# Statistics of the first 30 blocks summed on ACT and POOL, and the first pair's turn and keys ahead of the norm

## The chip, the core and the metric

The kernel runs on one core of one Trainium2 chip. The metric is the device time of one launch in microseconds (us), from start to end of the program on that core. Three runs of the kernel before took 2647.06, 2650.92 and 2656.12 us; the median is 2650.92. One further execution was recorded by the hardware profiler, and all views of the profile below come from it.

The engines are named as the profile names them: PE is TensorE (matmuls; PEld its weight loads), DVE is VectorE, ACT is ScalarE, POOL is GpSimd, and SP is SyncE, whose queue issues the transfers. Each engine runs its own instructions in order and waits on semaphores for the others.

## The reference

The input x has 256 rows of 256 positions of 128 channels. Two layers each add something to x. Only the head of the first one matters here:

```python
def _gn(v, G=32, eps=1e-5):
    B_, H_, W_, C_ = v.shape
    g = v.reshape(B_, H_, W_, G, C_ // G)
    m = jnp.mean(g, axis=(1, 2, 4), keepdims=True)
    s = jnp.var(g, axis=(1, 2, 4), keepdims=True)
    return ((g - m) / jnp.sqrt(s + eps)).reshape(v.shape)
...
q = split_heads(jnp.einsum('...qi,oi->...qo', q_x, wq)) / np.sqrt(C_HIDDEN)
k = split_heads(jnp.einsum('...ki,oi->...ko', kv_x, wk))
v = split_heads(jnp.einsum('...ki,oi->...ko', kv_x, wv))
a = jnp.einsum('bshqd,bshkd->bshqk', q, k)
a = a + bias1 + bias2
a = jax.nn.softmax(a, axis=-1)
...
x = x + _L0_conv_ref(_gn(x), L0_conv_kv_x, L0_conv_bias1, ...)
```

The group norm `_gn` needs the mean and variance of groups of 4 channels over all of x, 32 MB, before the first query can be made. Keys and values come from `kv_x` and need no norm. The second layer (an operator made of Fourier transforms, with norms of its own) follows on the result; the change doesn't touch it.

## The kernel before, in words

`layer0` does the first layer in two stages.

**Reading for the statistics.** x is read in 32 blocks of 1 MB (`xb`, line 140, four buffers; line 141 issues the transfer on SP). PE turns each block by transposes into four PSUM tiles of 128 channels by 512 (line 145, six buffers), and DVE takes a mean and a variance of each tile (`bn_stats`, line 146): 128 tiles in all, kept in `stats`. A tile's entry has six numbers: count, mean and sum of squared deviations of its even and of its odd elements. After block 2 the weights come: lines 148 to 153 issue their transfers on SP between those of the blocks (two buffers for the raw weights, so that SP waits for PE before it loads wv, wg and wo), PE transposes them (line 155) and ACT copies them. After block 8 `prepare` does the same with the two biases: bias1 is loaded into the still unused big array `U` (line 248), PE transposes it (line 255), ACT takes its exponential (line 259), POOL scales it (line 260). At the end `load` (line 277) issues the first two pairs of rows: eight transfers of 64 KB for each, four of x and four of kv.

**The norm.** DVE puts the 128 entries together (`bn_aggr`, line 166), a matmul with `gavg` averages over each group (line 50), ACT copies the mean (line 51), DVE works out the channel variances around it (lines 53 to 55), a second matmul averages those (line 57), ACT copies, and `rsqrt` follows: DVE adds eps (line 35), ACT takes a square root (line 37; a table of functions has to be loaded into ACT first), DVE inverts and improves it (lines 38 to 43). `fold` (lines 231 to 240) multiplies the query and gate weights with the result (`wn`, line 237) and makes their constants `qb` and `hbg` with two small matmuls (line 238).

**The loop over rows.** `run` writes the order of all engines out by hand: within `manual_schedule` each engine's instructions keep the order in which the program names them. Rows go in pairs. `turn` (line 303, DVE) transposes a pair of x and kv rows in squares of 32; `project` (PE line 295, ACT line 318) makes queries and keys of a row; `values` makes the values of a pair (ACT line 326) and the gate's sums; `gates` takes tanh (line 333); `scores` does the row's scores (PE line 343) and exponentials (ACT line 352); `weigh` multiplies with the bias (DVE line 368 for half of the heads, POOL line 370 for the others) and sums (POOL line 375); `attend` and `out` finish the row. The loop starts at i = -1, in which `project(0)`, `values(0)` with the gate's sums, and `turn(1)` are done; `gates(0)` then precedes row 0's scores.

Outside of `manual_schedule`, as in the reading, a scheduler orders each engine's instructions; the instructions on SP's queue stand roughly in the order of the program. A tile pool gives a buffer out again when the last reader of its old content is done.

Of the kernel before, what the change touches and what calls it, by code (L numbers as in the profile page):

```python
# [10 lines left out]
FP = mybir.dt.float32  # L11
AF = mybir.ActivationFunctionType
# [6 lines left out]
P = 128  # L19
# [87 lines left out]
def layer0(tc, I, C, ident, x1d, U, Q2, mv2, groups):  # L107
# [11 lines left out]
    with ExitStack() as ctx:  # L119
# [9 lines left out]
        adft = const.tile([P, 2, 129], FP, name="adft")  # L129

        rows = Rows(tc, I, rctx, x1d, U, Q2, mv2, wT, bg, adft, bad, ident)
        with tc.tile_pool(name="l0p", bufs=2) as pp, tc.tile_pool(
            name="l0pp", bufs=6, space=PSUM
        ) as ps_p:
            gavg = pp.tile([P, P], FP, name="gavg", bufs=1)
            stats = pp.tile([P, NS // 2, 6], FP, name="stats1", bufs=1)

            xr = x.rearrange("s q c -> (s q) c").rearrange("(b p n) c -> b p n c", p=P, n=16)
            for b in range(xr.shape[0]):
                xb = pp.tile([P, 16, P], FP, tag="xb", name=f"xb_{b}", bufs=4)  # L140
                nc.sync.dma_start(xb, xr[b])
                for t in range(4):
                    ps = ps_p.tile([P, 512], FP, tag="a", name=f"xps_{b}_{t}")
                    for k in range(4):
                        nc.tensor.transpose(ps[:, k * P : (k + 1) * P], xb[:, 4 * t + k, :], ident)
                    nc.vector.bn_stats(stats[:, b * 4 + t, :], ps)
                if b == 2:
                    nc.sync.dma_start(gavg, C["gavg"])
                    nc.sync.dma_start(bg, I["L0_conv_bg"].unsqueeze(1))
                    nc.sync.dma_start(adft, C["adft"].rearrange("(j p) f -> p j f", p=P))  # L150
                    for n in ("wq", "wk", "wv", "wg", "wo"):
                        w = pp.tile([P, P], FP, tag="w", name="w_" + n)
                        nc.sync.dma_start(w, I["L0_conv_" + n])
                        ps = ps_p.tile([P, 512], FP, tag="a", name="wps_" + n)
                        nc.tensor.transpose(ps[:, 0:P], w, ident)
                        wT[n] = const.tile([P, P], FP, name="wT_" + n)
                        if n in ("wq", "wo"):
                            nc.scalar.mul(wT[n], ps[:, 0:P], WO_SCALE if n == "wo" else 1.0 / math.sqrt(32.0))
                        else:
                            nc.scalar.copy(wT[n], ps[:, 0:P])  # L160
                if b == 8:
                    rows.prepare(pp, ps_p)
            rows.load(0)
            rows.load(1)
            mv = pp.tile([P, 2], FP, name="mv1", bufs=1)
            nc.vector.bn_aggr(mv, stats.rearrange("p a b -> p (a b)"))
            g = group_stats(nc, pp, ps_p, mv, gavg, "g1")
            nc.vector.tensor_copy(mr, g)
            rows.fold(ps_p, mr)

        rows.run()
        rctx.close()

        with tc.tile_pool(name="l0f", bufs=1) as fp, tc.tile_pool(
# [32 lines left out]
class Rows:  # L207
# [20 lines left out]
        self.b2T = const.tile([P, 2, self.NS], FP, name="b2T")  # L228
        self.rows, self.raw = {}, {}

    def fold(self, psum, mr):

        nc = self.tc.nc
        nc.vector.tensor_scalar(self.nm, mr[:, 0:1], -1.0, None, ALU.mult)
        ps = psum.tile([P, 512], FP, tag="a", name="foldps")
        for k, n in enumerate(("wq", "wg")):
            nc.vector.tensor_scalar(self.wn[n], self.wT[n], mr[:, 1:2], None, ALU.mult)
            nc.tensor.matmul(ps[:, k : k + 1], self.wn[n], self.nm, start=True, stop=True)
        nc.vector.tensor_copy(self.qb, ps[:, 0:1])
        nc.vector.tensor_scalar(self.hbg, ps[:, 1:2], self.bg, 0.5, ALU.add, ALU.mult)  # L240

    def prepare(self, bp, ps_b):
        nc, I, ident = self.tc.nc, self.I, self.ident
# [36 lines left out]
    def run(self):  # L280
# [1 line left out]
        nc = tc.nc  # L282
        ctx, wT, rows, raw = self.ctx, self.wT, self.rows, self.raw
        b1T, b2T, bad = self.b1T, self.b2T, self.bad
        wk = ctx.enter_context(tc.tile_pool(name="l0wk", bufs=2))
        ps_s = ctx.enter_context(tc.tile_pool(name="l0s", bufs=1, space=PSUM))
        ps_a = ctx.enter_context(tc.tile_pool(name="l0a", bufs=4, space=PSUM))
        pairs = {}
        turned = wk.tile([P, 6, 512], FP, name="turned", bufs=1)

        def by_columns(out, w, src, start=True, stop=True):

            for h in range(4):
                hd = slice(32 * h, 32 * h + 32)
                nc.tensor.matmul(out[hd], w[:, hd], src, start=start, stop=stop)  # L295

        def row(s):
            return pairs[s // 2], slice(256 * (s % 2), 256 * (s % 2) + 256)

        def turn(g):  # L300
            t = raw.pop(g)
            a, b = g % 4, 4 + g % 2
            nc.vector.transpose(  # L303
                turned[:, a : b + 1 : b - a].rearrange("p k (b c) -> p k b c", c=32), t
            )
            pairs[g] = {"xT": turned[:, a], "kvT": turned[:, b]}
            if g + 2 < NS // 2:
                self.load(g + 2)

        def project(s):  # L310
            p, q = row(s)
            ps = ps_a.tile([P, 512], FP, tag="a", name=f"qk_{s}")
            by_columns(ps[:, 0:256], self.wn["wq"], p["xT"][:, q])
            by_columns(ps[:, 256:512], wT["wk"], p["kvT"][:, q])
            r = rows[s] = {}
            r["qkT"] = wk.tile([P, 512], FP, tag="qkT", name=f"qkT_{s}")

            nc.scalar.activation(r["qkT"], ps, AF.Identity, bias=self.qb)  # L318

        def values(g):  # L320
            p = pairs[g]
            ps = ps_a.tile([P, 512], FP, tag="a", name=f"v_{g}")
            for c in range(4):
                by_columns(ps[:, c * P : (c + 1) * P], p["kvT"][:, c * P : (c + 1) * P], wT["wv"])
            p["v"] = wk.tile([P, 4, P], FP, tag="v", name=f"v_{g}")
            nc.scalar.copy(p["v"].rearrange("p c d -> p (c d)"), ps)
            p["g"] = ps_a.tile([P, 512], FP, tag="a", name=f"g_{g}")
            by_columns(p["g"], self.wn["wg"], p["xT"])

# [130 lines left out]
        def whole(k):  # L460
            return 0 <= k < NS // 2

        with tc.manual_schedule(engines={ENG.PE, ENG.Activation, ENG.DVE, ENG.Pool, ENG.SP}):
            turn(0)
            for i in range(-1, NS + 1):
                g, odd = i // 2, i % 2
                if odd and whole(g - 2):
                    again(g - 2)
                    squares(g - 2)
                if not odd and whole(g):  # L470
                    gates(g)
                if 0 <= i < NS:
                    scores(i)
# [2 lines left out]
                if 0 <= i < NS:  # L476
                    exp = rows[i].pop("exp")
                    exp(1, 0)
                    exp(1, 1)
                    weigh(i)  # L480
                if odd and whole(g + 1):
                    values(g + 1)
                if odd and whole(g + 2):
                    turn(g + 2)
                if not odd and whole(g - 2):
# [1696 lines left out]
```

## Time and profile before

| | |
|---|---|
| median of three runs | 2650.92 us (2647.06 to 2656.12) |
| the profiled execution's own time | 2650.27 us |
| its span | 2648.5 us |
| busy: PE | 2406.1 us (91%) |
| busy: DVE | 2032.0 us (77%) |
| busy: POOL | 1485.6 us (56%) |
| busy: ACT | 1420.4 us (54%) |
| mean granted clock of PE | 0.951 of full speed |
| first `bn_stats` of block 3 | 22.48 us |
| `bn_aggr` starts | 101.16 us |
| first exponential of row 0 | 119.72 us |
| last row's work on POOL (line 370) starts | 1424.0 us |

How to read the views: in the order of time, each line gives the start and the duration in us, the engine, the line of the kernel, the operation, what it writes and reads, the shapes, how many instructions were merged (x16), and in brackets how long the engine had been idle before and what ended that. In the stretches, each engine's busy us in the window stand with the number of instructions, then PE's granted clock (1.00 is full speed), the share of time that the 16 DMA engines were busy, and what they moved.

### The profile page before, as it was taken

How to read it: one execution, taken by the hardware profiler on the slowest of the kernel's cores; microseconds unless marked ns; L12 is line 12 of the kernel's file. 1: busy time of each engine (PE TensorE's matmuls, PEld its weight loads, DVE VectorE, ACT ScalarE, POOL GpSimd, SP SyncE). 2: the span in 40 equal slices, each digit the busy share in tenths (PEclk: the TensorE clock that was granted, in tenths of full speed). 3: DMA queues.
4: the chain of work that ended last, by engine and by line, in shares of the span. 5: the costliest groups of instructions: out<-in, count | busy, mean ns of one | idle time of the engine just before them, and what ended most of it. 6: DMA issues, size and time to landing. Idle time of an engine off the chain costs nothing. (4 is left out here: it accounts for less than half of the span.)

```text
span 2648.5 us, 88789 instructions
## 1 busy us (share of the span) xinstructions
PE 2406.1 (91%) x37586; PEld 1537.2 (58%) x37586; DVE 2032.0 (77%) x2883; ACT 1420.4 (54%) x2720; POOL 1485.6 (56%) x1041
## 2 busy tenths in 40 slices
PE   6699999999999999999998999998979888898754
PEld 6555655555565656565554567786754466454522
DVE  7799999999999999999997457566646654465455
ACT  0278888888888888888885122001016402555232
POOL 1199999999999999999995012002136412111211
PEclk9899999999999999999998999999989988999855
DMA  9655566566565656566563011888877755997699
GB/s 360 215 92 101 105 107 107 103 107 106 105 106 100 111 100 109 103 106 106 105 107 70 6 58 63 268 273 289 296 278 268 261 194 159 333 349 268 196 384 350
DMA packets 1016869, 458.49 MB, mean 173 GB/s; under 512 B 831062, under 2 KB 946217, under 8 KB 1010072
## 3 DMA queue, kind: packets, MB, share of 16 engines
q1 hardware_dynamic: 976664, 362.61, 54.7%
q0 software_dynamic: 22912, 81.80, 8.0%
q10 hardware_dynamic: 16896, 8.39, 1.1%
q8 instruction: 298, 4.88, 0.8%
q14 instruction: 99, 0.81, 0.1%
HBM read 317.36 MB, written 135.27 MB: 171 GB/s over the span
## 5 line engine op out<-in xcount | busy, mean ns | idle before, releaser
L370 POOL TENSOR_TENSOR e<-e,b1T 128x1024 f32<-128x1024 f32 x255 | 604.4, 2370 | 145.8 <-DMA xk<-in_L_conv_kv_x_dram 78.5
L375 POOL TENSOR_TENSOR es<-e 128x512 f32<-128x512 f32 x512 | 648.0, 1288 | 0.1
L397 DVE RECIPROCAL av<-av 128x256 f32<-128x256 f32 x256 | 452.2, 1766 | 9.1
L352 ACT ACTIVATE sc<-sc,b2T 128x512 f32<-128x512 f32 x514 | 340.0, 662 | 123.9 <-PE sc L343 111.8
L352 ACT ACTIVATE e<-sc,b2T 128x512 f32<-128x512 f32 x510 | 322.8, 693 | 0.0
L368 DVE TENSOR_TENSOR e<-sc,b1T 128x1024 f32<-128x1024 f32 x257 | 312.1, 1215 | 10.1 <-ACT sc L352 9.7
L343 PE MATMUL sc<-qkT 32*128 32x256 f32 x4096 | 293.7, 400 | 2.5 <-DVE e L368 2.5
L1440 PE MATMUL yps<-xt,mpT 128*128 128x256 f32 x1024 | 246.5, 391 | 31.8 <-DMA xt<-x1d 16.0
L385 PE MATMUL av<-e,v 128*32 128x256 f32 x4096 | 268.6, 379 | 1.8 <-DVE gate L398 1.7
L343 PEld LDWEIGHTS sc<-qkT 32*128 32x128 f32 x4096 | 185.7, 184 | 114.9 <-issue 52.3
L1440 PEld LDWEIGHTS yps<-xt,mpT 128*128 128x128 f32 x1024 | 192.0, 193 | 76.1 <-DVE yt L1452 20.2
L385 PEld LDWEIGHTS av<-e,v 128*32 128x32 f32 x4096 | 130.2, 110 | 125.8 <-issue 38.1
L1456 POOL DMA_DIRECT2D yd<-yt x32 | 17.4, 545 | 317.0 <-DVE yt L1452 311.1
L318 ACT ACTIVATE qkT<-qk,qb 128x512 f32<-128x512 f32 x256 | 174.0, 680 | 6.6 <-PE qk L295 6.5
L295 PE MATMUL qk<-turned,wn_wq 128*32 128x256 f32 x2048 | 164.0, 392 | 1.8 <-DVE turned L303 1.8
L442 ACT ACTIVATE turned<-turned 128x256 f32<-128x256 f32 x256 | 104.3, 408 | 112.1 <-DVE x1b L410 109.8
L390 PE MATMUL av<-es,ones 128*32 128x256 f32 x2048 | 160.7, 379 | 1.6 <-POOL es L375 1.6
L295 PEld LDWEIGHTS u<-adft,x 128*32 128x32 f32 x4096 | 118.5, 110 | 74.9 <-issue 74.7
L295 PE MATMUL qk<-turned,wT_wk 128*32 128x256 f32 x2048 | 157.9, 380 | 0.0
L303 DVE STREAM_TRANSPOSE turned<-xk 128x1024 f32<-128x1024 f32 x128 | 157.8, 1233 | 0.1
L1843 ACT ACTIVATE blocks<-h2ps,col 128x512 f32<-128x512 f32 x128 | 88.8, 778 | 128.1 <-PE h2ps L1307 128.1
L295 PE MATMUL u<-adft,x 128*32 128x129 f32 x4096 | 137.0, 273 | 0.0
(544 smaller groups left out, 4163.8 us busy)
## 6 DMA issues: line engine op xcount, KB each, us to landing
xt<-x1d SPq DMA_DIRECT2D x128, 512.0 KB, 6.6
xb<-in_x_dram SPq DMA_DIRECT2D x32, 1024.0 KB, 7.8
xk<-in_x_dram SPq DMA_DIRECT2D x512, 64.0 KB, 3.2
xk<-in_L_conv_kv_x_dram SPq DMA_DIRECT2D x512, 64.0 KB, 2.8
x1d<-x1b SPq DMA_DIRECT2D x512, 64.0 KB, 2.3
x<-x1d SPq DMA_DIRECT2D x126, 256.0 KB, 3.2
y<-yd SPq DMA_DIRECT2D x62, 512.0 KB, 7.1
gs<-Gd SPq DMA_DIRECT2D x384, 64.0 KB, 5.4
```

What stands on the lines that cost most here:

```text
L295: nc.tensor.matmul(out[hd], w[:, hd], src, start=start, stop=stop)
L303: nc.vector.transpose(turned[:, a : b + 1 : b - a].rearrange("p k (b c) -> p k b c", c=32), t)
L318: nc.scalar.activation(r["qkT"], ps, AF.Identity, bias=self.qb)
L343: nc.tensor.matmul(sc[h // 2][:, h % 2, c * 256 : (c + 1) * 256], qkT[p, 256 + c * P : 256 + (c + 1) * P], qkT[p, 0:256], start=True, stop ...
L352: nc.scalar.activation(r["e"][1][:, :, c, :] if hp and s < NS - 1 else z, z, AF.Exp, bias=b2T[:, c, s : s + 1])
L368: nc.vector.tensor_tensor(e, sc.rearrange("p h x -> p (h x)"), w, ALU.mult)
L370: nc.gpsimd.tensor_tensor(e, e, w, ALU.mult)
L375: nc.gpsimd.tensor_tensor(es, e[:, :, 0, :], e[:, :, 1, :], ALU.add)
L385: nc.tensor.matmul(ps[hd, 0:256], p["v"][:, 2 * (s % 2) + c, hd], r["e"][h // 2][:, h % 2, c, :], start=(c == 0), stop=(c == 1),)
L390: nc.tensor.matmul(ps[32 * h : 32 * h + 32, 256:512], self.ones, r["es"][h // 2][:, h % 2, :], start=True, stop=True,)
L397: nc.vector.reciprocal(rd, rd)
L1440: nc.tensor.matmul(rows_of(ps[j]), mpT[:, sc, tt], by_turn(xt[:, sc])[:, j], start=(sc == 0), stop=False,)
```

## The change

The sums of the first 30 of the 32 blocks are made while the last two are read; the rest of the norm is shorter; some work that doesn't need the norm is put ahead of it.

- `run` becomes a generator. `layer0` takes its steps between its own: buffers first, then `turn(0)` and `keys(0)`, then `project(0)` for the queries of row 0, then the rest.
- The blocks of x are read into five pieces of `U` instead of four buffers of their own. The PSUM buffers of the head go from six to four, because those of the rows (four) now exist beside them.
- Entries of blocks 0 to 29 are summed by three ACT operations with an accumulator (means against the first mean, their squares, the sums of squared deviations) and six small POOL operations. A square root on ACT, whose value isn't used, follows them. POOL also makes two scaled copies of `gavg` early.
- `bn_aggr` then sees only the last 8 entries. Each of the two averaging matmuls becomes two, one for either part of x. Copies from PSUM are made by DVE instead of ACT, or fall away.
- `turn(0)` and `keys(0)` stand between the second averaging matmul and the variance's square root.
- `fold` is split: the query weight first, then row 0's queries, then the gate's weight.
- In the loop, the keys of a row come ahead of its queries; the gate's sums are a step of their own (`gate`), for the first pair behind row 0's exponentials.

PE's order after the last transposes, as the program is built: the two pairs of averaging matmuls, four key matmuls (each instruction does two passes), one of the values of pair 0, the fold of wq, four query matmuls, the fold of wg, the other 15 of the values, the scores of row 0. On ACT: square root, qkT of row 0, the values' copy, a table load, the exponentials of row 0. On SP the fourth block's transfer (counting from 0) now stands ahead of the loads of wv and wg.

```diff
         rows = Rows(tc, I, rctx, x1d, U, Q2, mv2, wT, bg, adft, bad, ident)
+        steps = rows.run()
+        next(steps)
...
-            name="l0pp", bufs=6, space=PSUM
+            name="l0pp", bufs=4, space=PSUM
...
+            room = U.rearrange("p f s -> p (f s)")
...
-                xb = pp.tile([P, 16, P], FP, tag="xb", name=f"xb_{b}", bufs=4)
+                xb = room[:, 2048 * (1 + b % 5) : 2048 * (2 + b % 5)].rearrange("p (n c) -> p n c", c=P)
...
+                    for k, share in ((1, late / NB), (0, 1 - late / NB)):
+                        nc.gpsimd.tensor_scalar(gavg[:, k], gavg[:, 0], share, None, ALU.mult)
...
+                if b == NB - late - 1:
+                    early = stats[:, 0 : 4 * (b + 1)].rearrange("p b (h k) -> p (b h) k", h=2)
+                    n, flat = 8 * (b + 1), junk[:, 0 : 8 * (b + 1)]
+                    nc.gpsimd.tensor_scalar(col[:, 6:7], early[:, 0, 1:2], -1.0, None, ALU.mult)
+                    nc.scalar.activation(flat, early[:, :, 1], AF.Identity, bias=col[:, 6:7], accum_out=col[:, 7:8])
+                    nc.scalar.activation(
+                        flat, early[:, :, 1], AF.Square, bias=col[:, 6:7], accum_out=col[:, 8:9]
+                    )
+                    nc.scalar.activation(flat, early[:, :, 2], AF.Identity, accum_out=col[:, 9:10])
+                    nc.scalar.activation(col[:, 10:11], col[:, 9:10], AF.Sqrt)
+                    g = nc.gpsimd
+                    g.tensor_scalar(col[:, 7:9], col[:, 7:9], 1.0 / n, None, ALU.mult)
+                    g.tensor_tensor(col[:, 0:1], col[:, 7:8], col[:, 6:7], ALU.subtract)
+                    g.tensor_tensor(col[:, 7:8], col[:, 7:8], col[:, 7:8], ALU.mult)
+                    g.tensor_scalar(col[:, 9:10], col[:, 9:10], 1.0 / (256 * n), None, ALU.mult)
+                    g.tensor_tensor(col[:, 8:9], col[:, 8:9], col[:, 7:8], ALU.subtract)
+                    g.tensor_tensor(col[:, 2:3], col[:, 8:9], col[:, 9:10], ALU.add)
             rows.load(0)
             rows.load(1)
-            mv = pp.tile([P, 2], FP, name="mv1", bufs=1)
-            nc.vector.bn_aggr(mv, stats.rearrange("p a b -> p (a b)"))
-            g = group_stats(nc, pp, ps_p, mv, gavg, "g1")
-            nc.vector.tensor_copy(mr, g)
-            rows.fold(ps_p, mr)
-
-        rows.run()
+
+            last = pp.tile([P, 2], FP, name="mv1", bufs=1)
+            with tc.manual_schedule(engines={ENG.PE, ENG.Activation, ENG.DVE, ENG.Pool}):
+                nc.vector.bn_aggr(last, stats[:, 4 * (NB - late) :].rearrange("p a b -> p (a b)"))
+                nc.vector.tensor_copy(col[:, 1:4:2], last)
+                ps = ps_p.tile([P, 512], FP, tag="a", name="g1_ps")
+                for k in range(2):
+                    nc.tensor.matmul(ps[:, 0:1], gavg[:, k], col[:, k : k + 1], start=(k == 0), stop=(k == 1))
+                nc.vector.tensor_copy(mr[:, 0:1], ps[:, 0:1])
+                d = col[:, 4:6]
+                nc.vector.tensor_scalar(d, col[:, 0:2], mr[:, 0:1], None, ALU.subtract)
+                nc.vector.tensor_mul(d, d, d)
+                nc.vector.tensor_add(d, d, col[:, 2:4])
+                ps = ps_p.tile([P, 512], FP, tag="a", name="g1_ps2")
+                for k in range(2):
+                    nc.tensor.matmul(ps[:, 0:1], gavg[:, k], d[:, k : k + 1], start=(k == 0), stop=(k == 1))
+                next(steps)
+                rsqrt(nc, pp, mr[:, 1:2], ps[:, 0:1], EPS, "g1")
+                ps = ps_p.tile([P, 512], FP, tag="a", name="foldps")
+                rows.fold(ps, mr, "wq")
+                next(steps)
+                rows.fold(ps, mr, "wg")
+
+        for _ in steps:
+            pass
...
+        yield
+        turn(0)
+        keys(0)
+        yield
+        project(0)
+        yield
...
         with tc.manual_schedule(engines={ENG.PE, ENG.Activation, ENG.DVE, ENG.Pool, ENG.SP}):
-            turn(0)
-            for i in range(-1, NS + 1):
+            values(0)
+            turn(1)
+            for i in range(0, NS + 1):
...
+                if i == 0:
+                    gate(0)
+                    gates(0)
                 if odd and whole(g + 1):
                     values(g + 1)
+                    gate(g + 1)
```

## The prediction, on record before the run

> **What bounds the kernel now.** I read the profile's busy slices first, then the busy times by stretch of the first 250 us, then the order of time, because the change touches only what lies ahead of the loop over rows. Of the stretches (columns: busy us of each engine with its instructions, granted TensorE clock, DMA share, GB/s):
>
> ```profile
> core 0: us, PE busy (x) PEld busy (x) DVE busy (x) ACT busy (x) POOL busy (x), PEclk, DMA share, GB/s
> 30.00:40.00 10.00, 7.68 (x62) 6.38 (x60) 8.18 (x14) 2.42 (x5) 1.65 (x2) 1.00 0.96 361
> 60.00:70.00 10.00, 7.82 (x67) 7.00 (x66) 10.00 (x17) 0.00 (x0) 0.00 (x0) 1.00 1.02 424
> ...
> 100.00:110.00 10.00, 1.51 (x6) 1.00 (x4) 6.31 (x15) 1.80 (x4) 0.00 (x0) 0.50 0.32 51
> ...
> 200.00:250.00 50.00, 48.74 (x899) 28.63 (x899) 48.90 (x60) 38.98 (x80) 44.67 (x28) 1.00 0.59 102
> ```
>
> Three stages: reading x for the statistics (to about 100 us; DVE and DMA both full), a stretch in which no engine is full (100 to 119 us: a chain of small steps), and the loop, where PE is full (1098.74 of 1100 us between 200 and 1300). The loop starts when the chain ends, so each us taken from the first two stages moves the end by one. Order of time, first stage:
>
> ```profile
> 21.14 0.45 PE L155 MATMUL wps_wo<-ident,w_wo 128*128 128x128 f32 x1 [3.15 <-DMA w_wo<-in_L_conv_wo_dram]
> ...
> 22.48 0.70 DVE L146 BATCH_NORM_STATS2 stats<-xps 128x6 f32<-128x512 f32 x1 [7.53 <-PE xps L145]
> ...
> 25.90 12.28 DVE L146 BATCH_NORM_STATS2 stats<-xps 128x6 f32<-128x512 f32 x20 [0.15 <-PE xps L145]
> ...
> 36.92 1.94 PE L255 MATMUL b1ps<-ident,U 128*128 128x128 f32 x16 [1.62 <-DMA U<-in_L_conv_bias_dram]
> ...
> 40.80 9.95 DVE L146 BATCH_NORM_STATS2 stats<-xps 128x6 f32<-128x512 f32 x16 [2.63 <-PE xps L145]
> ...
> 59.09 37.27 DVE L146 BATCH_NORM_STATS2 stats<-xps 128x6 f32<-128x512 f32 x60 [0.33 <-PE xps L145]
> ...
> 97.45 2.95 PE L145 MATMUL xps<-ident,xb 128*128 128x128 f32 x16 [2.31 <-DMA xb<-in_x_dram]
> ```
>
> With work waiting, DVE takes (12.28-0.70)/19 = 0.609 us a tile; at the DMA's pace (37.27-0.70)/59 = 0.620. Losses: bubbles of 2.63 us at the bias transposes and 2.31 us of PE at the last block, smaller ones between. The last statistic ends at 100.43+0.70 = 101.13; call that T. Second stage, same view:
>
> ```profile
> 101.16 3.62 DVE L166 BATCH_NORM_AGGREGATE mv<-stats 128x2 f32<-128x768 f32 x1
> ...
> 105.53 0.16 ACT L51 COPY g_mr<-g_ps 128x1 f32<-128x1 f32 x1 [65.40 <-PE g_ps L50]
> ...
> 107.18 1.28 ACT L37 ACT_TABLE_LOAD   x1
> ...
> 111.78 2.37 DVE L303 STREAM_TRANSPOSE turned<-xk 128x1024 f32<-128x1024 f32 x2
> ...
> 113.17 1.08 PE L295 MATMUL qk<-turned,wn_wq 128*32 128x256 f32 x8 [1.80 <-DVE turned L303]
> ...
> 114.84 1.97 PE L295 MATMUL v<-wT_wv,turned 128*32 128x128 f32 x32
> ...
> 116.55 1.97 PE L295 MATMUL g<-turned,wn_wg 128*32 128x512 f32 x8
> ...
> 117.47 1.28 ACT L333 ACT_TABLE_LOAD   x1
> ...
> 118.45 1.23 PE L343 MATMUL sc<-qkT 32*128 32x256 f32 x16
> ...
> 119.72 1.36 ACT L352 ACTIVATE sc<-sc,b2T 128x512 f32<-128x512 f32 x2 [0.27 <-PE sc L343]
> ...
> 122.97 2.36 POOL L370 TENSOR_TENSOR e<-e,b1T 128x1024 f32<-128x1024 f32 x1 [78.50 <-DMA xk<-in_L_conv_kv_x_dram]
> ```
>
> First exp at T+18.59. After 122.97 POOL runs nearly without pause (127.78, 132.81, 137.60), so what precedes it is pure delay.
>
> **Part 1, five buffers for x.** Until now block 4's transfer stood on SP behind the wv and wg loads, which wait for PE, and went out at 15.64; with a fifth buffer it goes out once block 1 has landed (about 9). DMA fell to 49 to 250 GB/s between 13 and 18 us, so this fills a hole, and every later transfer, the bias among them, goes out one block earlier. PE's wait for wo (21.14) stays: wo still follows one block, now block 5. So statistics resume at 22.48 and finish block 8 at 38.18 as before. Then the bias transposes: their 1.62 us wait for U goes, but four PSUM buffers instead of six let DVE keep less in hand; I take a bubble of 2.0 (1.7 to 2.6). From 40.2 the 92 remaining tiles have data waiting: DMA leads by about four blocks and loses only 4x(0.620-0.609) = 0.04 us of it a block. End 40.2 + 91x0.609 + 0.70 = 96.3 at best; 38.18+2.63+91x0.620+0.70 = 97.9 at worst. I take 96.7: T falls by **4.4** (3.2 to 4.8). The row transfers (xk) also go out earlier, between the last blocks; the 2.31 us that they seem to cost at the end falls into the lead. Without the lead it stays.
>
> **Part 2, sums of 30 blocks on ACT and POOL.** Three ACT operations of 128x240, nearest row the 128x256 Square, 0.41+0.19: 1.8 us; table load 1.28 and Sqrt 0.20; then POOL, nearest row its 128x1 copy, 0.185: six operations, with hand-over some 0.35 each. They start when block 29 is done, T-8x0.61 = T-4.9. ACT ends at T-1.5, POOL's last two follow at about T-0.8; the first use is at T+0.6, the last needed column at T+2.3. Cost nothing; hidden by the last eight statistics. Were POOL 1 us an operation, the sums would come 1 to 2 us late. The two gavg scalings (128x128, a quarter of the 1.49 of L260) and POOL's early negation lie in its idle time before 38 us. The Trainium skill speaks against the place: "GPSIMD Engine Reference", Key points, has POOL share its SBUF interfaces with VectorE. The row: beside POOL's four scalings of b1T (38.27 to 44.47) the statistics ran at (9.95-0.70)/15 = 0.617. By the row nothing; by the rule, if all six stopped DVE, 1.1 us. I take nothing and keep 1.1 for the range.
>
> **Part 3, T to the first exp.** In us after T; gaps as in the chain before.
> - bn_aggr of 8 tiles: 3.62x48/768 = 0.23, plus a small instruction's 0.15: ends 0.4 (from 0.25 to 0.6). Copy to col: 0.6.
> - Two matmuls instead of one: 0.56+0.42 (spacing of the two folds): 1.7. DVE copy (no ACT hop) and three small steps of 0.2: 2.5. Two more matmuls: 3.6.
> - New on DVE ahead of the variance: the first pair's turn, 1.24, from 2.5 to 3.8: 0.2 late for L35. It waits for eight xk transfers, the last issued when the last block lands (T-3) and down 2.6 later, before 2.5. Queued behind it on DVE is the whole norm. Keys (8 matmuls, 1.1) and one v matmul run on PE from 3.9 to 5.2, while ACT and DVE finish rstd.
> - Sqrt without table load at 4.0; reciprocal and four steps: 5.15. wn_wq, nm: 5.6. Fold 5.7 to 6.25 (one weight, not two); qb 6.5.
> - PE: q alone 6.2 to 7.2; qkT on ACT 7.25 to 7.95. PE: fold of wg 0.5, v 0.94x1.97 = 1.8: 9.5. This is late next, not qkT. v's copy ends 10.1; table load 1.28: 11.4. Scores 9.5 to 10.7, hidden under it. First exp **11.4**.
> - The gate (0.69 on ACT, 1.97 on PE) moves behind row 0's exps: its ACT slot, 14.7 to 15.4, lies where ACT waits anyway for row 1's scores (0.87 idle before); nothing.
>
> Gain 18.6-11.4 = 7.2; I take **7.1** (6 to 8). turn(1), from 8.0, reads xk down by about T+5. Closing the head's PSUM pool makes scores wait for hbg (8.0), earlier than v.
>
> The second rule: PE's clock. The row: 0.50 from 99 to 117, and already 0.80 in 97 to 99 after a pause of 2.3 us; 1.00 from 119 on. "TensorE: Matmul & The Clock Gate", Part 1, says the clock falls after about 3.4 us idle; the new chain has no pause above 1.3 us, so by the rule PE stays at full clock and v and q need about half: 1.7 us more gain. The row saw it fall after less, so I keep the cold durations.
>
> **Loop.** Same instructions; of each projection the keys now precede q. At 700 us both take 0.64 and 0.61: no difference expected.
>
> Sum: 4.4+7.1 = 11.5. The profiled execution took 2650.27 (span 2648.5, 1.8 around it), 0.65 below the median 2650.92: 2650.27-11.5 = **2638.8**.
>
> **Rivals.**
> - The reading stays paced by DMA (2.484 us a block from 58.4 to 93.2; xk issued earlier spoil the lead): T moves by under 1, gain 7.1: 2643.2. For it: DMA share 1.02; against: the hole at 13 to 18. 0.14.
> - Sums or turn(0) late, that is, the change does not do what it says: ACT's wait on DVE may count later statistics, a thing the trace of before cannot show. With the 1.8+1.5+2.1 us of Part 2 begun at T, 4.8 of the 11.5 go: 2643.6. 0.07.
> - PE stays warm: 2637.1. 0.06.
> - Slower: the loop. PE is the bound there, and the switch from 32-row scores to 32-column projections now falls on the keys. If keys first exposed a weight load (0.11 us) in each of 255 rows, 28 us come, less 11.5: 2667. It decides from 11.5/255 = 45 ns a row. Against: the first group of eight pays 0.03 more already, whichever it is. 0.03.
>
> **How the numbers follow.** The forecast, own range 2635 to 2643, has 0.70. A measurement here tells about 0.3% from no change: 8 us, 2643.0. Faster: 0.70, plus 0.06 warm, plus a third of the first two rivals: 0.83. Same 0.14, slower 0.03. The range 2634 to 2645 takes in the unknown costs, the warm case and the DMA-paced one.
>
> **What would show it.** Right: last statistic near 96.7, bubble at the bias about 2, no DMA wait of PE late in the reading; aggregate under 0.6 us; ACT's second table load before T; the turn inside the norm; first exp near T+11.4; 5.1 us a row in the loop. Wrong: PE waiting for xb at 60 to 95, L200 waiting for POOL, the turn waiting for xk, or rows longer than 5.1.

## The result, and the profile after

The changed kernel took **2644.9 us** (median of 21 runs, 2634.2 to 2654.15) beside 2651.04 us (21 runs, 2647.06 to 2661.24) for the kernel before. The ratio is 0.9975, with a 95% interval from 0.9965 to 0.9985: 4.0 to 9.3 us faster. The profiled execution took 2646.19 us (span 2644.4). The forecast was 11.5 us of gain, 2638.8 us; about half of it came, and the median lies 0.1 us inside the end of the stated range of 2634 to 2645. One run of a kernel tried below, that of before with five pieces, took 4735.26 us where its other 21 took 2645.98 to 2674.6, and is left out of its median and ratio.

The order of time of the kernel after, first stage, beside the lines shown of before:

```profile
21.09 0.45 PE L161 MATMUL wps_wo<-ident,w_wo 128*128 128x128 f32 x1 [2.47 <-DMA w_wo<-in_L_conv_wo_dram]
...
22.42 0.70 DVE L152 BATCH_NORM_STATS2 stats<-xps 128x6 f32<-128x512 f32 x1 [6.74 <-PE xps L151]
...
39.68 54.68 DVE L152 BATCH_NORM_STATS2 stats<-xps 128x6 f32<-128x512 f32 x88 [1.87 <-PE xps L151]
...
41.52 1.94 PE L151 MATMUL xps<-ident,U 128*128 128x128 f32 x16 [0.56 <-DMA U<-in_x_dram]
...
91.19 1.94 PE L151 MATMUL xps<-ident,U 128*128 128x128 f32 x16 [0.54 <-DMA U<-in_x_dram]
91.97 0.63 ACT L175 ACTIVATE junk<-stats,col 128x240 f32<-128x240 f32 x1 [52.30 <-DVE stats L152]
...
94.09 1.28 ACT L180 ACT_TABLE_LOAD   x1
...
95.11 2.49 DVE L152 BATCH_NORM_STATS2 stats<-xps 128x6 f32<-128x512 f32 x4 [0.76 <-PE xps L151]
95.98 0.19 POOL L187 TENSOR_TENSOR col<-col 128x1 f32<-128x1 f32 x1
```

The bias bubble has shrunk to 1.87 us, and after it DVE goes through 88 tiles in one piece. But its pace there is (54.68-0.70)/87 = 0.6205 us a tile, the DMA's pace of before, and PE waits 0.53 to 0.56 us for DMA ahead of every block from 41.52 (block 10, the second behind the bias) to 91.19. The last statistic ends at 95.11+2.49 = 97.60 (T; 101.13 in the profile of before). The early sums start when block 29 is done and end on POOL at 96.17, 1.4 us ahead of T. Second stage, same view:

```profile
97.64 0.37 DVE L193 BATCH_NORM_AGGREGATE mv<-stats 128x2 f32<-128x48 f32 x1
...
99.80 0.58 PE L205 MATMUL g_ps<-col,gavg 128*128 128x1 f32 x4 [1.14 <-DVE col L202]
...
99.89 1.25 DVE L346 STREAM_TRANSPOSE turned<-xk 128x1024 f32<-128x1024 f32 x1 [0.24 <-DMA xk<-in_L_conv_kv_x_dram]
...
101.06 0.12 DVE L35 TENSOR_SCALAR g_ve<-g_ps 128x1 f32<-128x1 f32 x1
...
101.21 0.20 ACT L37 ACTIVATE g_r<-g_ve 128x1 f32<-128x1 f32 x1 [5.62 <-DVE g_ve L35]
...
103.40 1.08 PE L338 MATMUL qk<-turned,wn_wq 128*32 128x256 f32 x8
...
104.92 1.93 PE L338 MATMUL v<-wT_wv,turned 128*32 128x128 f32 x30
...
106.78 2.09 PE L396 MATMUL sc<-qkT 32*128 32x256 f32 x16
106.91 0.58 ACT L376 COPY v<-v 128x512 f32<-128x512 f32 x1 [1.68 <-PE v L338]
107.51 1.28 ACT L405 ACT_TABLE_LOAD   x1
108.91 1.36 ACT L405 ACTIVATE sc<-sc,b2T 128x512 f32<-128x512 f32 x2
110.81 0.69 ACT L368 ACTIVATE qkT<-qk,qb 128x512 f32<-128x512 f32 x1 [0.54 <-PE qk L338]
111.39 1.26 ACT L405 ACTIVATE e<-sc,b2T 128x512 f32<-128x512 f32 x2
...
112.78 2.36 POOL L423 TENSOR_TENSOR e<-e,b1T 128x1024 f32<-128x1024 f32 x1 [16.60 <-ACT e L405]
```

The first exponential starts at 108.91 = T+11.31, and POOL's first multiplication with the bias at 112.78, 10.2 us earlier than before. Does the loop keep these? The tile `e` on POOL, before and after (shortest, median and longest duration in ns, then the first and the last start):

```profile
L370 POOL TENSOR_TENSOR e<-e,b1T x255: 2352/2371/2385, 123.0 to 1424.0; 128x1024 f32<-128x1024 f32 x128
```

```profile
L423 POOL TENSOR_TENSOR e<-e,b1T x255: 2359/2371/2388, 112.8 to 1413.8; 128x1024 f32<-128x1024 f32 x128
```

It does: 1301.0 us from first to last in both, and the last row is 10.2 us earlier. From there to the end of the span, nearly all of it code that the change doesn't touch, it is 1224.5 us before and 1230.6 after. So these two executions differ by 10.2 us at the end of the rows and by 4.1 at the end. The experiments ask first which of the two numbers is the change's, and then where the missing part of the 11.5 is.

### The profile page after: what moved, and what is told of

It reads as the page before. It is cut to its first block, busy times and chain, and to the rows that moved or that the text cites. A ratio compares the mean times of both kernels' runs of the same rounds, so it can differ in the third digit from the quotient of the medians.

```text
span 2644.4 us, 88819 instructions
## 1 busy us (share of the span) xinstructions
PE 2420.7 (92%) x37590; PEld 1544.6 (58%) x37590; DVE 2029.4 (77%) x2884; ACT 1422.5 (54%) x2725; POOL 1488.5 (56%) x1050
## 5 line engine op out<-in xcount | busy, mean ns | idle before, releaser
L338 PE MATMUL qk<-turned,wT_wk 128*32 128x256 f32 x2048 | 164.5, 393 | 0.8 <-DVE g_ve L35 0.8
L338 PE MATMUL qk<-turned,wn_wq 128*32 128x256 f32 x2048 | 158.3, 381 | 0.0
## 6 DMA issues: line engine op xcount, KB each, us to landing
U<-in_x_dram SPq DMA_DIRECT2D x32, 1024.0 KB, 10.3
```

## Experiments

Two kinds of kernel: whole ones, timed against the kernel before on the same chip, and cut ones, which end after the first layer. The table gives medians; intervals are at each run below.

| kernel | chip | us (runs) | before, whole | ratio |
|---|---|---|---|---|
| changed kernel again | 6 | 2651.45 (22) | 2657.61 | 0.9979 |
| four pieces of `U` | 6 | 2650.57 (22) | 2657.61 | 0.9979 |
| values behind row 0's exps | 6 | 2649.66 (22) | 2657.61 | 0.9979 |
| kernel before, five pieces | 6 | 2660.86 (21) | 2657.61 | 1.0009 |
| three idle `bn_aggr` added | 14 | 2656.43 (22) | 2654.0 | 1.0011 |
| before again | 14 | 2652.58 (14) | 2654.0 | 1.0002 |
| before, cut | 14 | 1451.37 (5) | | |
| after, cut | 14 | 1442.49 (5) | | |
| before with five pieces, cut | 0 | 1448.73 (5) | | |
| early sums undone, cut | 0 | 1446.55 (5) | | |
| turn and keys late, cut | 0 | 1446.5 (5) | | |
| values late, cut | 0 | 1441.43 (5) | | |

The last four cut kernels ran on another chip than the two that they are compared with. Their differences of medians could hold a difference between chips, so each is set beside the traces below, stretch by stretch: T, from T to POOL's first multiplication, the loop, and what follows.

**The changed kernel once more**, no edit.

> The changed kernel once more, to see how its second layer varies. Call L the time from the start of the last row's POOL multiplication to the end of the span: 1224.5 us in the profile of before, 1230.6 in that of after. Theory N (the second layer has the same instructions and only scatters from run to run): L lies anywhere between 1221 and 1231, and the gain over before over many runs comes near the 10 us that the head has saved. Theory S (the second layer is really longer after the change, which gives back some 4 us): L again near 1230 and the gain again near 6. Both: the last statistic ends at 97.6, first exponential at 108.9.

2651.45 us, ratio 0.9979 (0.9963 to 0.9994), so 1.6 to 9.8 us faster. In its profile POOL's rows run from 113.1 to 1417.7: the loop took 1304.6 us in this execution, and the stretch behind it 1239.5, 9 more than in the first profile of the same program. That stretch scatters by more than the question asks.

**Four pieces of `U` instead of five**, the rest of the change kept.

```diff
-xb = room[:, 2048 * (1 + b % 5) : 2048 * (2 + b % 5)].rearrange("p (n c) -> p n c", c=P)
+xb = room[:, 2048 * (1 + b % 4) : 2048 * (2 + b % 4)].rearrange("p (n c) -> p n c", c=P)
```

> The changed kernel with four pieces of U in place of five: the fifth buffer taken away, the rest kept. Theory R (the 3.5 us by which the reading ends earlier come from the fifth buffer: the block that fills the hole at 13 to 18 us, the bias one block earlier): the last statistic ends at 100.5 to 101.2, the first exponential 11.3 after that. Rival P (they come from four PSUM buffers and the schedule of the head): it stays near 97.6. For L: N 1221 to 1231, S near 1230.

0.9979 (0.9966 to 0.9992). By the time it is not told from the changed kernel. Its profile tells it apart: T is 100.74, as before the change, and the first exponential comes at T+11.3. In the order of time (PE and DVE at the last block):

```profile
97.58 1.94 PE L151 MATMUL xps<-ident,U 128*128 128x128 f32 x16 [2.10 <-DMA U<-in_x_dram]
98.25 2.49 DVE L152 BATCH_NORM_STATS2 stats<-xps 128x6 f32<-128x512 f32 x4 [1.55 <-PE xps L151]
100.78 0.37 DVE L193 BATCH_NORM_AGGREGATE mv<-stats 128x2 f32<-128x48 f32 x1
```

PE's wait for the last block, 2.10 us, is about as long as before (2.31); the short norm is untouched by it. The fifth piece and the short norm are two separate gains.

**The kernel before with five pieces**, nothing else of the change.

```diff
+room = U.rearrange("p f s -> p (f s)")
...
-xb = pp.tile([P, 16, P], FP, tag="xb", name=f"xb_{b}", bufs=4)
+xb = room[:, 2048 * (1 + b % 5) : 2048 * (2 + b % 5)].rearrange("p (n c) -> p n c", c=P)
```

> The kernel before with five pieces of U in place of its four buffers for x, and nothing else of the change; six PSUM buffers stay. Theory R: the last statistic ends at 97.4 to 98.0 instead of 101.1, the first exponential 18.6 after that, and the kernel is 3 to 3.5 us faster (0.9987). Rival P: 100 to 101, same time. For L: N 1221 to 1231, S (whatever in the change lengthens it is not the reading) near 1225.

1.0009 (0.9993 to 1.0025): not told from no change. In its profile T is 98.63, between what the two theories expected. A whole kernel can't resolve two us; the cut one below can.

**Values of the first pair behind row 0's exponentials.**

```diff
-            values(0)
             turn(1)
...
                 if i == 0:
+                    values(0)
                     gate(0)
```

> The changed kernel with the values of the first pair behind row 0's exponentials instead of ahead of its scores. In the profile of after, the 30 value matmuls (104.92 to 106.85) and their copy (0.58) stand between the queries and the table load, and the first exponential starts at T+11.3. If they are what ends last there, as the prediction had it: scores start at T+7.9, the table load right behind qkT, the first exponential at T+9.5 to 10, and POOL's first multiplication 1.3 to 1.8 us earlier than 112.8. If the table load or the cold clock is what ends last, less than 0.5 us earlier. For L: N 1221 to 1231, S near 1230.

0.9979 (0.9965 to 0.9993), the changed kernel's ratio. In its profile the first exponential comes at T+9.9 instead of T+11.3, so the edit does what it says, but the loop of that one execution took 1316.9 us instead of 1301.0 (its cut twin below has 1301.0 again). Inconclusive by the whole time.

**Both kernels without the second layer.** In both, `layer1` is replaced by a copy of two rows.

```diff
-        layer1(tc, I, C, ident, x1d, held, U, Q2, g2, out)
+        nc.sync.dma_start(out[0:2], x1d[0:2].rearrange("s h w -> (s h w)").rearrange("(s h w) -> s h w", h=out.shape[1], w=out.shape[2]))
+        held.release_now()
```

> The kernel before without its second layer; only two rows of the sum after the first layer are copied to the output, so the output is not the reference's. It is timed to be compared with the same cut of the changed kernel, next to it on the same chip. By the profile of before, the last row's POOL work starts at 1424.0; both theories: about 1435 to 1445 us, with a spread from run to run that shows how much of the whole kernel's spread comes from the second layer.

> The changed kernel without its second layer, cut in the same way (output not the reference's). Theory N and theory S both: faster than the cut kernel before by the 10.2 us of the profiles (1424.0 against 1413.8), and then what is missing in the whole kernel, 10.2 less about 6, is lost behind the rows. Theory H (executions without a profile gain less in the head than the profiled one): faster by only 6.

1451.37 us (1450.74 to 1451.44) and 1442.49 us (1441.40 to 1442.84): **8.9 us**, between the 10.2 and the 6 of the theories. (The 1435 to 1445 expected for the first was too low: 25.7 us follow the start of its last row's POOL work, at 1423.9.) The runs of these two lie within 0.7 and 1.4 us (those of the other cut kernels within 1.6 to 4.5), the runs of whole kernels within 12 to 29: most of the scatter belongs to the second layer. The two profiled executions, of which that of after is the fastest of its five, differ by 10.0: T 2.15 (100.25 against 98.10), from T to POOL's first multiplication 6.85 (21.45 against 14.60), the loop 1.2 (1302.2 against 1301.0), and 0.2 less behind it. The first layer alone gives 8.9, not 11.5; the forecast was too large by 2.6 before the second layer begins.

**Does the second layer take something back?** Three unused `bn_aggr` of all entries, 3.62 us each, ahead of the short one push the changed kernel's loop to where that of before starts, or a bit later. If the changed program loses time in the second layer whatever its head does, it must now be clearly slower than before.

```diff
+                pad = pp.tile([P, 2], FP, name="pad", bufs=1)
+                for _ in range(3):
+                    nc.vector.bn_aggr(pad, stats.rearrange("p a b -> p (a b)"))
                 nc.vector.bn_aggr(last, stats[:, 4 * (NB - late) :].rearrange("p a b -> p (a b)"))
```

> The changed kernel with three more aggregates of all 128 entries, 3.62 us each, on DVE ahead of the short one; their results aren't used. They put 10.9 us back into the norm's chain, so the rows start at 123.7, 0.7 later than before. Theory S1 (something in the changed kernel itself makes the second layer some 4 us longer, whenever it starts): 4 to 5 us slower than before (1.0017). Theory S2 (the second layer doesn't follow the start one for one; begun at the old time it takes the old time): same as before, 0 to 1 us slower. Theory N (scatter): same as before as well.

> The kernel before against itself: the ratio is 1.000, and what it shows beside that is how far two sets of runs of one kernel differ. A second profile for L: theory N 1221 to 1240 like those of the changed kernels on this kind of chip (1228.3 to 1239.5 so far), theory S near 1225.

The delayed kernel: 1.0011 (0.9999 to 1.0022), 2.9 us slower by the ratio, 2656.43 against 2654.0. From its order of time:

```profile
99.12 10.94 DVE L195 BATCH_NORM_AGGREGATE pad<-stats 128x2 f32<-128x768 f32 x3
109.97 0.31 DVE L196 BATCH_NORM_AGGREGATE mv<-stats 128x2 f32<-128x48 f32 x1
```

Its first multiplication on POOL starts at 125.3, 2.3 to 3.6 us later than in three profiles of before (123.0, 121.8, 121.7). So its head, 3.5 us later than in the two profiles of before on the same chip, explains the 2.9; no further loss is left over, though the interval (-0.3 to 5.8) doesn't exclude one of 2 us. Before against itself gave 1.0002 (0.9987 to 1.0017). The stretch from the last row to the end, over eight whole profiles: 1224.5, 1234.8 and 1236.6 with the norm of before (before twice, and with five pieces); 1230.6, 1239.5, 1228.3, 1231.5 and 1227.8 with that of after (after twice, four pieces, values late, delayed). The ranges overlap, and the means are 1232.0 and 1231.5. A fixed loss of about 4 us in the second layer is not supported.

**The fifth piece alone, cut.** The edit of the whole one, and the second layer left out.

> The kernel before with five pieces of U for x (nothing else of the change), cut behind the rows like the other two cut kernels (output not the reference's). The cut kernels took 1451.37 (before) and 1442.49 (after). Theory A (the reading gives 2 to 2.5 of the 8.9 us, not the 4.4 of the forecast: the profiled execution of before had a slow head, its last statistic at 101.1 against 100.1 and 100.3 in two later ones): 1448.9 to 1449.4. Rival B (the reading does give about 4, and the chain less than 7): 1447 to 1447.5.

1448.73 us (1447.61 to 1449.18), 2.6 less than the cut kernel before. The traces of the two show that it is the reading: T is 97.84 instead of 100.25, 2.4 earlier, and everything else is equal to 0.1 us (T+21.46 and T+21.45 at POOL, loops of 1302.3 and 1302.2, 25.7 behind them). The rest, 1448.73-1442.49 = 6.2 by the medians, belongs to Parts 2 and 3.

**The early sums undone, cut.** One `bn_aggr` of all 128 entries takes the place of the three ACT and six POOL operations, and each average is one matmul again; the early square root, which brings the table in, is kept.

```diff
-                    nc.scalar.activation(flat, early[:, :, 1], AF.Identity, bias=col[:, 6:7], accum_out=col[:, 7:8])
...
-                    g.tensor_tensor(col[:, 2:3], col[:, 8:9], col[:, 9:10], ALU.add)
+                    nc.scalar.activation(col[:, 10:11], stats[:, 4 * b, 2:3], AF.Sqrt)
...
-                nc.vector.bn_aggr(last, stats[:, 4 * (NB - late) :].rearrange("p a b -> p (a b)"))
+                nc.vector.bn_aggr(last, stats.rearrange("p a b -> p (a b)"))
```

> The changed kernel without the early sums: all 128 entries in one aggregate at the end, one matmul for each average; everything else of the change is kept, the early Sqrt table too. Cut behind the rows (output not the reference's). If the early sums save the aggregate's 3.62-0.37 us less a copy (0.22) and the second matmuls (0.1 to 0.3 each): 2.4 to 2.8 us over 1442.5, so 1444.9 to 1445.3. If they were late or hidden anyway: 1442.5.

1446.55 us (1445.76 to 1448.8), 4.1 more than after, where less was expected. Its order of time:

```profile
97.56 1.94 PE L151 MATMUL xps<-ident,U 128*128 128x128 f32 x16 [1.56 <-DMA U<-in_x_dram]
...
100.75 3.62 DVE L176 BATCH_NORM_AGGREGATE mv<-stats 128x2 f32<-128x768 f32 x1
...
107.30 0.12 DVE L35 TENSOR_SCALAR g_ve<-g_ps 128x1 f32<-128x1 f32 x1
...
114.79 1.28 ACT L385 ACT_TABLE_LOAD   x1 [1.05 <-PE sc L376]
116.08 1.36 ACT L385 ACTIVATE sc<-sc,b2T 128x512 f32<-128x512 f32 x2
```

The long aggregate costs 3.25 us more than the short one. The table load, which in the changed kernel ran beside the scores, comes after them here, and a wait of 1.05 us stands ahead of it. From T (100.72) to the first exponential this makes 15.4 instead of 11.3. The sums account for 3.1 of these 4.1: so much stands already at line 35 (T+6.58 instead of T+3.46), since the second matmuls that the sums cost were hidden beside the turn. The other 1.0 is the table load's new place, which the expectation didn't have and for which no run shows the cause. That the medians differ by 4.1 too is partly chance: T was 2.6 later in this execution than in that of the cut kernel after.

**Turn and keys behind the fold of wq, cut.**

```diff
-                next(steps)
                 rsqrt(nc, pp, mr[:, 1:2], ps[:, 0:1], EPS, "g1")
...
                 rows.fold(ps, mr, "wq")
                 next(steps)
+                next(steps)
```

> The changed kernel with the first pair's turn and keys behind the fold of wq instead of inside the norm. Cut behind the rows (output not the reference's). The turn (1.25) and its hand-over come back into the chain ahead of the queries, and the keys (8 matmul passes, 1.08 in the cold) stand ahead of them on PE: 1.9 to 2.4 us over 1442.5, so 1444.4 to 1444.9. If the values and the table load were what ended last whatever the queries do, half of that or less.

1446.5 us (1444.08 to 1448.53), 4.0 more than after. In its order of time:

```profile
99.63 0.37 DVE L193 BATCH_NORM_AGGREGATE mv<-stats 128x2 f32<-128x48 f32 x1
...
105.77 1.25 DVE L346 STREAM_TRANSPOSE turned<-xk 128x1024 f32<-128x1024 f32 x1 [0.21 <-issue]
...
113.05 1.36 ACT L405 ACTIVATE sc<-sc,b2T 128x512 f32<-128x512 f32 x2
```

The first exponential is at T+13.5 instead of T+11.3: 2.2 us, as expected. At POOL it is 2.1 (T+16.71 instead of T+14.60). T is 99.6 in this execution, 1.5 later than in that of the cut kernel after, and its loop is 1.1 longer (1302.1). The runs of this kernel spread by 4.5 us, and whether any of the 1.8 beyond the chain belongs to the edit isn't settled.

**Values late, cut.** The edit shown above, without the second layer.

> The kernel with the first pair's values behind row 0's exponentials, cut behind the rows (output not the reference's); the whole kernel's comparison could not tell its gain from the scatter of the second layer. Its first profile had the first exponential at T+9.9 instead of T+11.3 and POOL's first multiplication at T+13.6 instead of T+15.2. If that carries through to the end of the rows: 1.4 to 1.6 us under 1442.5, so 1440.9 to 1441.1. If POOL or PE of the first rows takes it back: 1442 to 1442.5.

1441.43 us (1440.85 to 1442.68), 1.1 less than after; the ranges overlap. What ends last now:

```profile
106.48 1.28 ACT L405 ACT_TABLE_LOAD   x1
...
108.67 1.36 ACT L405 ACTIVATE sc<-sc,b2T 128x512 f32<-128x512 f32 x2 [0.90 <-PE sc L396]
```

The table load is done early, and ACT waits 0.90 us for the scores, which take 2.09 us on a PE at half clock: the first exponential is at T+10.1, not earlier. At POOL's first multiplication 0.75 us of the 1.2 are left (T+13.85 instead of T+14.60). It has the lowest median of the cut kernels, but a gain of this size isn't settled, and the whole kernel doesn't show it.

## Why the prediction was half right

**The direction held, and the mechanism of the chain.** The two gains, an earlier T and a shorter chain behind it, are there, each by the part of the change that was named for it. How the fifth buffer brings the first, the forecast had wrong.

**Part 1 is where the forecast failed, in two of its steps.** It forecast that T falls by 4.4 us (3.2 to 4.8). In the two profiles T falls by 3.5, inside that range, but this is luck: of the 14 profiles of this study that of before has the latest T and that of after the earliest. With four buffers (before, before again, before cut, and the changed kernel with four pieces) T was 101.13, 100.12, 100.25 and 100.74, mean 100.6; with five it lay between 97.60 and 100.72, mean 98.8. So T moves by 1.7 on average, and by about as much within one chip (100.12 and 100.25 against 98.10 and 99.09; 100.74 against 98.63, 98.62 and 99.52). Half a us of the luck can be seen: PE's clock fell during the last block of the profile of before (the line at 97.45: 2.95 us, where 12 of the other 13 profiles have 1.94), and its statistics end 3.68 us after that line's start, in after 3.15.

*"With a fifth buffer it goes out once block 1 has landed (about 9)."* Block 4 did go out early, but the fifth buffer was not the reason. Its transfer on SP's queue: in the kernel before; in before with five pieces, cut; in the changed kernel with four pieces; in the changed kernel (x2: blocks 3 and 4, ahead of wv and wg):

```profile
15.64 0.42 SPq L141 DMA_DIRECT2D xb<-in_x_dram  x1
```

```profile
14.71 0.42 SPq L142 DMA_DIRECT2D U<-in_x_dram  x1
```

```profile
5.65 4.12 SPq L147 DMA_DIRECT2D U<-in_x_dram  x2
```

```profile
5.63 2.84 SPq L147 DMA_DIRECT2D U<-in_x_dram  x2
```

With five pieces alone it still stands behind wv and wg; with the rest of the change it goes out ahead of them with four pieces too. It is the order of SP's queue in the changed program that fills the hole. And the filled hole is not what moves T. Busy time by stretch, 13 to 18 us and 60 to 90 us (granted clock, DMA share and GB/s at the end of the line), first before, then after:

```profile
13.00:15.00 2.00, 0.54 (x2) 0.28 (x2) 1.95 (x4) 0.20 (x1) 0.00 (x0) 1.00 0.50 201
15.00:18.00 3.00, 0.66 (x2) 0.35 (x2) 0.00 (x0) 0.48 (x3) 0.00 (x0) 0.71 0.60 161
...
60.00:90.00 30.00, 23.43 (x196) 20.90 (x194) 29.98 (x49) 0.00 (x0) 0.00 (x0) 1.00 1.01 422
```

```profile
13.00:15.00 2.00, 1.61 (x13) 1.18 (x11) 2.00 (x4) 0.37 (x2) 0.00 (x0) 1.00 1.02 426
15.00:18.00 3.00, 0.00 (x0) 0.00 (x0) 0.68 (x2) 0.18 (x1) 0.00 (x0) 1.00 1.00 344
...
60.00:90.00 30.00, 23.44 (x196) 20.96 (x195) 30.00 (x50) 0.00 (x0) 0.00 (x0) 1.00 1.02 421
```

From 13 to 18 us the kernel after moved 0.426x2+0.344x3 = 1.88 MB and the one before 0.201x2+0.161x3 = 0.89. But the changed kernel with four pieces moved 1.8 MB there, and its T was 100.74; the two profiles of before with five pieces moved 0.9 and 1.4 MB, no more than those of before (0.9 to 1.4), and their T was 98.63 and 97.84. Over the 14 profiles the data moved from 13 to 18 us hardly go with T (correlation -0.30). What goes with T is all that was moved from 0 to 44 us (mean GB/s of that stretch times 44): correlation -0.93, from 14.5 MB and T = 101.13 in the profile of before to 15.6 MB and 97.60 in that of after, 2.8 us for each MB (1 MB takes 2.4 at 421 GB/s). From about 38 us on the transfers are saturated in both kernels (421 and 422 GB/s from 38 to 44 us), so what is missing then is missing at T.

What the fifth piece adds comes behind the hole. The two cut kernels that differ in nothing else, first four buffers, then five:

```profile
13.00:22.00 9.00, 2.90 (x17) 2.47 (x16) 2.56 (x5) 1.18 (x5) 0.00 (x0) 0.73 0.89 328
22.00:32.00 10.00, 9.53 (x74) 8.84 (x72) 9.54 (x17) 0.00 (x0) 0.00 (x0) 0.90 0.85 300
32.00:44.00 12.00, 8.49 (x60) 8.20 (x61) 6.83 (x13) 2.98 (x5) 4.73 (x4) 0.86 0.98 382
```

```profile
13.00:22.00 9.00, 2.93 (x18) 2.40 (x17) 2.44 (x5) 1.24 (x5) 0.00 (x0) 0.77 0.81 302
22.00:32.00 10.00, 9.89 (x76) 9.32 (x74) 9.54 (x16) 0.00 (x0) 0.00 (x0) 0.87 1.00 380
32.00:44.00 12.00, 8.64 (x72) 7.82 (x73) 9.89 (x17) 2.54 (x5) 5.96 (x4) 1.00 1.04 412
```

From 22 to 32 us DVE is busy for 9.54 of 10 us in both; with four buffers the DMA engines are not (0.85), with five they are (1.00). One more place to put a block keeps the transfers going while the statistics are behind. By 44 us this comes to 15.5 instead of 14.6 MB, 2.2 us at 421 GB/s, and T moved by 2.4. A whole block more (1.05 MB) would be 2.5 us, an estimate from the same rate.

*"From 40.2 the 92 remaining tiles have data waiting: DMA leads by about four blocks."* No lead formed: in the profile of after PE waits for the DMA from the second block behind the bias on (41.52), and the tiles take 0.6205 us instead of 0.609, which is 1.0 us over 91 tiles. The last block stays late, as the forecast said for the case without a lead: DVE waits 0.74 to 1.47 us for it in the profiles with five pieces, 1.21 to 1.75 in those with four. So five pieces end at 98.8 on average, not at 96.7. That is 2.1 of the 2.7 us by which the forecast was too large; the other 0.6 is the late T of the one profile of before. Why three of the ten executions with five pieces moved only 14.7 to 14.8 MB by 44 us, with T at 99.5 to 100.7, **stays open**.

This was the first rival, right in that the DMA paces the reading. Its reason was not: the first xk goes out at 83.60, long after the waits begin. Its time, 2643.2, is nearer than the forecast's; its "T moves by under 1" was too little.

**Part 2 held.** ACT's three operations took 0.63, 0.61 and 0.52 us plus 0.19 each for reading the accumulator, somewhat above the 0.41+0.19 of the nearest row; POOL's six took 0.19 to 0.23. They ended 1.4 us ahead of T (forecast 0.8) and cost nothing that the trace shows: the run of 88 tiles, which ends beside them at 94.36, kept 0.6205 us a tile. The 1.1 us that the forecast held ready did not follow from "GPSIMD Engine Reference", Key points: that line speaks of DVE instructions in a 2-port mode or with two SBUF inputs, and the statistics read one tile, from PSUM. Without the sums the chain is 3.1 us longer up to line 35.

**Part 3 held at the first exponential.** Forecast T+11.4, measured T+11.31; before T+18.59 (18.4 and 18.2 in later profiles). The steps, forecast against the trace: aggregate end 0.4 and 0.41; turn 2.5 to 3.8 and 2.3 to 3.5; square root 4.0 and 3.6; end of the fold 6.25 and 5.9; end of v 9.5 and 9.25; end of the table load 11.4 and 11.2. Two details were off. The scores took 2.09 instead of the 1.23 of the row, since PE's clock came back later than theirs; they end at 108.87, level with the table load, so that v and the scores bind together. And from the first exponential to POOL's first multiplication it takes 3.87 us instead of 3.25: row 1's queries were still made at half clock, and ACT waited 0.54 us for them (the line at 110.81) ahead of row 0's second pair of exponentials. That belongs to this execution: in two other profiles of the changed kernel (again, and cut) it takes 3.3 and 3.2. At POOL the chain is shorter by 6.7 in the pair of profiles and by 6.8 on average (T+21.6 in five profiles with the old norm, T+14.8 in four with the new one), against 7.1 forecast.

**The clock.** By the rule that the forecast weighed, from "TensorE: Matmul & The Clock Gate", Part 1 (a fall after an idle window of about 3.4 us), PE should have stayed at full clock through the new chain. It had no pause above 1.8 us between 94 and 104, and yet, in the stretches of the kernel after, the granted clock fell:

```profile
97.00:99.00 2.00, 0.38 (x2) 0.30 (x2) 1.34 (x6) 0.00 (x0) 0.00 (x0) 1.00 0.78 125
99.00:101.00 2.00, 0.58 (x4) 0.52 (x4) 1.62 (x4) 0.00 (x0) 0.00 (x0) 0.90 0.70 110
101.00:103.00 2.00, 1.58 (x11) 0.68 (x11) 1.32 (x9) 0.20 (x1) 0.00 (x0) 0.50 0.35 56
```

A PE that was busy for 0.38+0.58 of 4 us, with no long pause, lost its clock all the same. To keep the cold durations was right, and the rival of the warm PE fell.

**The loop held**: 1301.0 us in both, 1302.2 and 1301.0 in the two cut kernels, and nothing of the slower case, which asked for 28 us. (Three other profiles have longer loops, 1304.3 in the kernel before with five pieces, 1304.6 and 1316.9 in the two named above; they are on both sides and not tied to an edit.)

**The sum.** By the traces: T 1.7 (mean of all) to 2.4 (the fifth piece alone), chain 6.8, together 8.5 to 9.2, against 4.4+7.1; the first layer's measured 8.9 lies in it. The whole kernel gained 6.6 by the ratio (4.0 to 9.3), and 5.6 (1.6 to 9.8) when it was run again. Both intervals hold 8.9 and neither holds 11.5. Put together as independent they give about 6.3 (4.1 to 8.5, an estimate from the two intervals), which 8.9 (7.9 to 10.0 by the ranges of the cut kernels) only just meets. Whether the two or three us between are scatter, or are given back in the second layer by something that depends on when it starts, **stays open**: that stretch varies by 15 us over eight profiles, the delayed kernel shows no fixed loss, and no run resolved it further.

## What to carry to other kernels

In a stage that the DMA paces, count all the bytes that are moved by the time the transfers are saturated; filling one hole early may leave another behind it. A fifth 1 MB buffer was worth at most its block at the stage's rate (2.5 us; 1.7 to 2.4 came), and no lead grew where the reader was as fast as the transfers. Take the start of a chain from several executions, or from what paces it, before a few us of it are booked as gain. And where the tail of a program scatters by more than the change is worth, cut the tail off and time the rest: here that turned an uncertainty of 5 us into one of 2.

## What the runs showed of the hardware that was not expected

With one more 1 MB block in flight, the median from issue to landing of a block went from 7.8 to 10.3 us, while the saturated rate stayed at 422 and 421 GB/s: there the queue got longer, not faster. PE's granted clock fell to half in a stretch of short pauses, none above 1.8 us, and was full again only at about 111 us, after 7 us in which PE was busy almost without a pause (from 103.4). ACT took 0.52 to 0.63 us for 128x240 numbers of which it reads every third, longer than its 0.41 for 128x256 in the trace of before; that the stride is the cause was not tried.
